# Four quarters of an MLP projection by seven products instead of eight, in a cross-attention kernel on one core

## The chip, the core and the metric

The kernel runs on one core of one Trainium2 chip. Such a core has TensorE (PE, the matmul array), VectorE (DVE), ScalarE (ACT), GpSimd (POOL) and SyncE (SP), which in this kernel only issues DMAs. Each engine runs its own instructions in the order in which the program gives them, and waits on semaphores for what others make. SBUF holds tiles of 128 partitions, PSUM the results of matmuls in eight banks of 128x512 fp32.

The metric is the device time of one execution in microseconds (us). A profile is one execution recorded by the hardware. Its span is the time between the first and the last recorded instruction, somewhat less than the time of the execution.

## The reference

One transformer block of cross-attention and MLP, in fp32, for 4 batches of 512 rows of 512 features, a context of the same shape, and 16 heads of 32 features:

```python
x = layer_norm(hidden_states, ln1_w, ln1_b)
q = x @ q_w + q_b ; k = ctx @ k_w + k_b ; v = ctx @ v_w + v_b      # 16 heads of 32
attn = softmax(where(mask, q @ k.T / sqrt(32), min))
hidden = (attn @ v) @ cproj_w + cproj_b + hidden_states
y = layer_norm(hidden, ln2_w, ln2_b)
return hidden + gelu(y @ fc_w + fc_b) @ proj_w + proj_b            # 512 -> 2048 -> 512
```

## The kernel before

**Units and blocks.** The attention is cut into 16 units w, each a batch (w // 4) and a group of four heads, and each unit into two halves of 256 query rows: 32 blocks p, and with each a pair (unit, half) of softmaxes. `block` runs eight score products (`scores`, line 317), then for each of them `soften`: VectorE reads the scores from PSUM and finds the extreme value (line 323), ScalarE takes exp (line 327). VectorE transposes the results (`turn`, line 335), takes reciprocals of the sums (line 354), ScalarE spreads them (`rr`, line 356) and VectorE transposes them too (line 360). `exchange` then moves the pair between partitions, by four GpSimd copies (line 393) and twelve DMAs on SP's queue (line 398), as soon as the buffer is free. `attend` of that pair (32 products of line 415) runs two blocks later, ahead of that block's scores.

**Fills.** VectorE and ScalarE need longer for a block's softmax than TensorE for its scores. So the list `put(p, ...)` gives each block other TensorE work, which `fill` issues at three points of the block: the first two take what fits in a budget of `CHAIN` = 3.4, the third takes all that is left. Such work is K, Q and V of later units (`prep_k`, line 255; `prep_q`, line 267; `prep_v_pair`, line 298), the output projection `cproj` (line 455), and the MLP of batches 0 and 1, taken in the order of the list `products` by `some(n)`. After the blocks come the last projection of the attention and what is left of the MLP.

**The MLP.** `fc` makes 2048 hidden features in pairs of 128, each pair by seven products over blocks of 128x256 (`fc_seven`, line 646; Strassen's scheme in Winograd's form, which saves one of eight products and adds sums of operands and results). Sums of fc's weights are made by GpSimd ahead of time (`fc_sums`, lines 597 and 600). The gelu of a pair (line 667) isn't issued with the pair but put into a list, `S["gelu"]`, that is emptied later: by the next pair's products, by a `proj` that needs it, or behind the `rr` copy of a block that has no pair in it. `proj` takes the hidden features in four quarters q of 512; each quarter has four row tiles t, of four matmuls 128x512 each, whose result VectorE adds to the row tile of the residual (line 709):

```python
for k in range(FQ):
    nc.tensor.matmul(acc, gT[q % 2][:, k, ts(t, P)], S["pw", b, q * FQ + k], ...)
h = S["hid", b, t]
nc.vector.tensor_tensor(h, acc, h, ALU.add)
```

Batch 1's first two quarters run by the same `proj`; the rest of the MLP runs behind the blocks.

**Weights.** `ptt` has twelve slots of 128x512: six for score tiles (`score_tile`), and six for the weights of K, Q and V, two slots for each (`kqv_w`); `load_w(w + 2)` follows a unit's last use of a slot. `pbt` holds eight weights of the MLP in turn, for which `load_mlp` (line 589) issues DMAs in the order of the list `weights`, as slots come free. All of these go through SP's queue, in the order of the program, like the DMAs of the exchange; a DMA that waits for its slot holds up those behind it. `store_rn` and `load_rn` (line 213) send the two rows of the layer norm's statistics through HBM and spread them over the partitions.

Of the kernel before, what the change touches and what calls it, by code (L numbers as in the profile page):

```python
# [20 lines left out]
P = 128  # L21
# [8 lines left out]
NQ = 4  # L30
# [4 lines left out]
FIRST = 2  # L35
IN_G = (1, 3, 5, 7)
IN_XE = (25, 27, 29, 31)

BY_ROW = ((1, 1), (1, 3))
BY_ACT = ((1, 2),)  # L40
# [11 lines left out]
def xattn_block(ctx: ExitStack, tc: tile.TileContext, x, rawT, encT, mask, q_w, k_w, v_w, c_w, fc_w, p_w, vecs, rows, out):  # L52
# [6 lines left out]
    const, keep, hids, tiles, small = pools(ctx, const=1, keep=1, hids=4, tiles=4, small=4)  # L59
# [28 lines left out]

    ys = const.tile([P, 3, 2, L // 2], F32, tag="ys", name="ys")
    wsum = const.tile([P, 2, 3, 2, P], F32, tag="wsum", name="wsum")  # L90

    def k_q(w, i):
        n = w % 4 * 2 + i
# [15 lines left out]
        return ptt[:, n * D : (n + 2) * D]  # L109

    def kqv_w(w, i):
        n = 4 * i + 2 + w % 2
        return ptt[:, n * D : (n + 1) * D].rearrange("p (d f) -> p d f", d=ND)

    S = {"gelu": []}
# [92 lines left out]
            )  # L208

    def load_rn(b):  # L210
        S["rows", b] = [hids.tile([P, L], F32, tag="hid2", bufs=2, name=f"rn_{b}_{i}") for i in range(2)]
        for i in range(2):
            nc.sync.dma_start(out=S["rows", b][i], in_=S["rn", b][i : i + 1, :].broadcast_to([P, L]))

# [25 lines left out]
    def load_w(w, queue=None, names=("wk", "wq", "wv")):  # L240
# [4 lines left out]
        for i, (n, src) in enumerate((("wk", k_w), ("wq", q_w), ("wv", v_w))):  # L245
            if n in names:
                S[n, w] = kqv_w(w, i)
                (queue or Q[0]).dma_start(out=S[n, w], in_=src[:, g, :, :])

    def prep_k(w):  # L250
        b, g = divmod(w, NG)
        kT = k_q(w, 0)
        acc = acc_tile(f"acck_{w}")
        for d in range(ND):
            nc.tensor.matmul(acc, S["wk", w][:, d, :], eT[:, d, :], start=(d == 0), stop=(d == ND - 1))  # L255
        load_w(w + 2, names=("wk",))
        nc.scalar.activation(kT, acc, AF.Identity, bias=vec[:, KB + g : KB + g + 1], scale=1.0)
        S["kT", w] = kT

    def prep_q(w):  # L260
        b, g = divmod(w, NG)
        qT = k_q(w, 1)
        parts = [slice(0, L)] if w else [slice(0, 2 * P), slice(2 * P, L)]
        for c in parts:
            acc = acc_tile(f"accq_{w}_{c.start}")[:, c]
            for d in range(ND):
                nc.tensor.matmul(acc, S["wq", w][:, d, :], xT[:, d, c], start=(d == 0), stop=(d == ND - 1))  # L267
            nc.scalar.activation(qT[:, c], acc, AF.Identity, bias=qb[:, g : g + 1], scale=-scale)
        load_w(w + 2, names=("wq",))
        S["qT", w] = qT  # L270

    def prep_v(w):
# [12 lines left out]
        if w:  # L285
            v_bias(w)

    def prep_v_pair(w):
        pair = range(w, w + 2)
        for u in pair:  # L290
            S["v", u] = five.tile([P, NT, P], F32, tag="v", name=f"v_{u}")
        n = 10
        wv = ptt[:, n * D : (n + 2) * D].rearrange("p (g d f) -> p d g f", g=2, d=ND)
        for i in range(2):
            acc = acc_tile(f"accv_{w}_{i}").rearrange("p (t g f) -> p t g f", t=2, g=2)
            for t in range(2):
                for d in range(ND):
                    nc.tensor.matmul(  # L298
                        acc[:, t], eT[:, d, ts(2 * i + t, P)], wv[:, d], start=(d == 0), stop=(d == ND - 1)
                    )  # L300
            for g, u in enumerate(pair):
                nc.scalar.copy(S["v", u][:, 2 * i : 2 * i + 2], acc[:, :, g])
        for u in pair:
            load_w(u + 2, names=("wv",))
            v_bias(u)

    def v_bias(w):
        v, bias = S["v", w], row[:, 2, ts(w % NG, P)]
# [123 lines left out]
    def load_h(b, *ts_):  # L432

        if ("xa", b) not in S:
            S["xa", b] = dram.tile([L, D], F32, tag=f"xa{b}", name=f"xa{b}")
        for t in ts_:
            if b == B - 1:

                S["h", b, t] = k_q(t // 2, t % 2)
            else:  # L440
                pool, tag, n = (tiles, "xn", 4) if not stays(b, t) else (hids, "hid2", 2) if b else (hids, "hid", 4)
                S["h", b, t] = pool.tile([P, D], F32, tag=tag, bufs=n, name=f"h_{b}_{t}")
# [93 lines left out]
    def load_hid(b, ts_):  # L536

        for t in ts_:
            if ("hid", b, t) not in S:
                S["hid", b, t] = hids.tile([P, D], F32, tag="hid", name=f"hid_{b}_{t}")  # L540
# [24 lines left out]
    def fcs(b, *cs):  # L565
        return [("fc", b, c) for c in cs]

    def pjs(b, q, *ts_):
        return [("p", b, q, t) for t in ts_ or range(NT)]
# [8 lines left out]
    weights = [(*k, n) for k, n in last_use.items()]  # L578

    weights += [("p", SPLIT, FIRST * FQ + k, None) for k in range(MW)]  # L580

    def load_mlp():

        while count[0] < len(weights) and (count[0] < MW or weights[count[0] - MW][3] < count[1]):
            name, b, f, _ = weights[count[0]]
            w = mlp_w(count[0])
            if name == "fc":
                w = w.rearrange("p (d f) -> p d f", d=ND)
            Q[0].dma_start(out=w, in_=fc_w[:, f, :, :] if name == "fc" else p_w[ts(f, P), :])
            S[name + "w", b, f] = w  # L590
            count[0] += 1

    NP = NF // 2
# [104 lines left out]
        count[4] += 1  # L698
        load_mlp()

    def proj(b, q, t):
        gelus(q % 2)
        acc = acc_tile(f"accp_{b}_{q}_{t}")
        for k in range(FQ):
            nc.tensor.matmul(  # L705
                acc, gT[q % 2][:, k, ts(t, P)], S["pw", b, q * FQ + k], start=(k == 0), stop=(k == FQ - 1)
            )
        h = S["hid", b, t]
        nc.vector.tensor_tensor(h, acc, h, ALU.add)
        if q == NQ - 1:  # L710
            (nc.gpsimd if b == 0 else nc.sync).dma_start(out=out[b, ts(t, P), :], in_=h)
# [25 lines left out]
    def last_mlps():  # L737
# [197 lines left out]
        for b, pairs, new in (  # L935
# [43 lines left out]

            project(b, pairs, sums, turns, middle)  # L980
            if b == SPLIT:
                S["more"] = [hids.tile([P, D], F32, tag="hid2", bufs=2, name=f"more_{n}") for n in range(2)]
                S["more"] = [m.rearrange("p (c n) -> p c n", c=NP // 2) for m in (*S["more"], row[:, 2, :])]
                to_split.extend(w_sums(5, pt[:, 2]))


# [3 lines left out]
    def do(fn):  # L990
        return [(0.0, fn)]
# [10 lines left out]
            (CHAIN, lambda: prep_v(w)),  # L1002
        ]

    def V(w):
        return [(CHAIN, lambda: prep_v_pair(w))]

    def C(b):
        return [(CHAIN, lambda t=t: cproj(b, t)) for t in range(NT)]
# [63 lines left out]
    def some(n):  # L1073
# [4 lines left out]
        assert n == 0  # L1078
        return taken

    def hid_(b, *ts_):
        return do(lambda: load_hid(b, ts_))

# [20 lines left out]
    def put(p, *work, before=(), mid=()):  # L1104
# [54 lines left out]
    put(26, c[3:], do(lambda: attend(12, 0)), some(2))  # L1159
    put(27, some(3))  # L1160
    put(28, some(3))
    put(29, some(4))
    put(30, some(3), hid_(1, 2, 3))
    put(31, some(3))

    due = {p: (p - 2,) for p in range(10, 2 * NW)}
    due |= {p: (p - 3,) for p in range(3, 9)} | {9: (6,), 26: ()}
    for p in range(2 * NW):
        w, half = divmod(p, 2)
        if half == 0 and w and w % NG == 0:  # L1170
            make_mb(w // NG)
        run(ahead[p])
        for pair in due.get(p, ()):
            attend(*divmod(pair, 2))
        if p > 10:
            fc_sums()

        def fill(n, work=fills[p]):
# [70 lines left out]
```

## Time and profile before

| | us |
|---|---|
| median of 3 runs | 762.17 (761.72 to 762.34) |
| the profiled execution, its own time | 760.67 |
| its span | 758.9 |
| TensorE busy | 753.9 |
| VectorE busy | 613.4 |
| GpSimd busy | 339.7 |
| ScalarE busy | 337.6 |

The page of the profile names instructions by line of the kernel (L705 is line 705), engine, operation and tile: `accp<-pbt,gt` is the product of `proj` from weights in `pbt` and hidden features in `gt`. In a timeline or in the chain of waits the first column is the start and the second the length in us; "x32" is the number of records; an fp32 matmul leaves two. A bracket at the end of a row holds the idle time of the engine ahead of the instruction, and what ended it. In the rows of the DMA queues "SPq" is the issue of a DMA by SP, not its transfer.

### The profile page before, as it was taken

To read this page: it belongs to the slowest core of one execution; us is meant where nothing else is said; L and a number is where in the kernel's file an instruction comes from. 1 tells how busy PE (TensorE), PEld (TensorE's weight loads), DVE (VectorE), ACT (ScalarE), POOL (GpSimd) and SP (SyncE) were. 2 spreads that over 40 slices of the span, in tenths; PEclk is the share of its full clock that TensorE was granted. 3 is DMA by queue.
4 is the path that set the end of the run, shared out by engine and by line. 5 is a ranking of instruction groups with operands and counts; after the bars stand their busy time and mean duration, and the time that the engine had idled before them with its cause. 6 is when DMAs were issued, how large, how long until landed. Compare 5 with 4: busy or idle time off the path is not lost.

```text
span 758.9 us, 13040 instructions
## 1 busy us (share of the span) xinstructions
PE 753.9 (99%) x4418; PEld 517.8 (68%) x4418; DVE 613.4 (81%) x1222; ACT 337.6 (44%) x768; POOL 339.7 (45%) x352
## 2 busy tenths in 40 slices
PE   9999999999999999999999999999999999999998
PEld 6655555567574545475454566468888899988997
DVE  3889999879995777887887989949877986956865
ACT  2566766565873574647753567501302221022200
POOL 1549447368664873244575444432050004403153
PEclk9999999999999999999999999999999999999999
DMA  9989889467897776665756867776724402046001
GB/s 329 341 255 247 207 207 257 104 199 200 220 243 229 223 231 177 184 175 129 177 133 186 214 194 193 172 227 215 260 98 135 167 26 91 30 146 214 1 15 43
DMA packets 60577, 134.59 MB, mean 177 GB/s; under 512 B 11312, under 2 KB 17072, under 8 KB 60384
## 3 DMA queue, kind: packets, MB, share of 16 engines
q1 hardware_dynamic: 58448, 126.73, 58.4%
q0 software_dynamic: 1920, 7.01, 2.7%
q8 instruction: 35, 0.57, 0.3%
q14 instruction: 30, 0.25, 0.1%
q10 hardware_dynamic: 144, 0.02, 0.0%
HBM read 69.23 MB, written 11.02 MB: 106 GB/s over the span
## 4 chain that ended last, share of the span: by engine, by line
PE 99%; POOL 0%; issue 0%; DVE 0%; DVEq 0%; POOLq 0%
PE q L646 26%; PE accp L705 11%; PE r L792 10%; PE sc L317 8%; PE av L415 8%; PE acck L255 8%; PE accq L267 8%; PE accc L455 6%; PE accv L278 5%; PE accv L298 3%; PE q1p L853 2%; PE tp L166 1%; PE warm L1044 1%; PE q3p L835 0%; PE q5p L835 0%; PE q4p L835 0%
## 5 line engine op out<-in xcount | busy, mean ns | idle before, releaser
L327 ACT ACTIVATE ptt<-ptt,mn 128x512 f32<-128x512 f32 x256 | 181.7, 711 | 142.8 <-DVE mn L323 142.8
L323 DVE CUSTOM_DVE_ANT_0 ptt<-sc,mb 128x512 f32<-128x512 f32 x256 | 160.6, 682 | 19.9 <-PE sc L317 19.8
L335 DVE STREAM_TRANSPOSE tb<-ptt 128x1024 f32<-128x1024 f32 x128 | 153.3, 1217 | 0.0
L393 POOL COPY pT<-tb 32x1088 f32<-32x1088 f32 x96 | 104.5, 1089 | 83.5 <-DVE oT L420 34.6
L705 PE MATMUL accp<-pbt,gt 128*128 128x512 f32 x192 | 85.3, 596 | 0.0
L646 PE MATMUL q<-yT,gt 128*128 128x256 f32 x320 | 78.9, 379 | 0.0
L667 ACT ACTIVATE ga<-ga,vec 128x512 f32<-128x512 f32 x40 | 26.7, 714 | 93.3 <-DVE ga L600 93.3
L646 PEld LDWEIGHTS q<-yT,gt 128*128 128x128 f32 x320 | 60.8, 190 | 8.1
L705 PEld LDWEIGHTS accp<-pbt,gt 128*128 128x128 f32 x192 | 35.9, 190 | 44.6 <-issue 39.1
L317 PE MATMUL sc<-pbt 32*128 32x512 f32 x512 | 64.7, 614 | 0.0
L646 PE MATMUL q<-ys,gt 128*128 128x256 f32 x240 | 61.6, 379 | 0.0
L255 PE MATMUL acck<-xe,ptt 128*128 128x512 f32 x128 | 59.0, 604 | 0.0
L267 PE MATMUL accq<-xe,ptt 128*128 128x512 f32 (+1 forms) x136 | 58.4, 575 | 0.0
L646 PEld LDWEIGHTS q<-ys,gt 128*128 128x128 f32 x240 | 45.7, 190 | 6.1
L600 DVE TENSOR_TENSOR ga<-q,ga 128x512 f32<-128x512 f32 (+1 forms) x60 | 36.2, 603 | 16.3 <-PE q L646 13.5
L327 ACT ACTIVATION_READ_ACCUMULATOR ptt<-ptt,mn 128x1 f32 x256 | 47.8, 187 | 0.0
L415 PE MATMUL av<-pT,v 128*32 128x256 f32 x768 | 46.4, 382 | 0.0
L267 PEld LDWEIGHTS accq<-xe,ptt 128*128 128x128 f32 x136 | 24.9, 190 | 31.4 <-issue 22.8
L255 PEld LDWEIGHTS acck<-xe,ptt 128*128 128x128 f32 x128 | 23.8, 193 | 30.8 <-issue 24.0
L317 PEld LDWEIGHTS sc<-pbt 32*128 32x128 f32 x512 | 26.9, 184 | 24.8 <-issue 16.9
L455 PE MATMUL accc<-wc,oT 128*128 128x512 f32 x96 | 42.5, 598 | 0.0
L278 PEld LDWEIGHTS accv<-ptt,xe 128*128 128x128 f32 x320 | 37.0, 192 | 4.9 <-DVE mn L323 2.7
(231 smaller groups left out, 1270.4 us busy)
## 6 DMA issues: line engine op xcount, KB each, us to landing
pT<-tb SPq DMA_DIRECT2D x288, 136.0 KB, 2.4
pbt<-p_w_dram SPq DMA_DIRECT2D x40, 256.0 KB, 3.3
gt<-ws SPq DMA_DIRECT2D x20, 512.0 KB, 3.3
gt<-tb SPq DMA_DIRECT2D x48, 136.0 KB, 3.8
xe<-tb SPq DMA_DIRECT2D x48, 136.0 KB, 2.5
pbt<-fc_w_dram SPq DMA_DIRECT2D x24, 256.0 KB, 4.7
gt<-fc_w_dram SPq DMA_DIRECT2D x20, 256.0 KB, 3.3
ptt<-k_w_dram SPq DMA_DIRECT2D x16, 256.0 KB, 4.2
```

The costliest lines, as they stand in the source:

```text
L255: nc.tensor.matmul(acc, S["wk", w][:, d, :], eT[:, d, :], start=(d == 0), stop=(d == ND - 1))
L267: nc.tensor.matmul(acc, S["wq", w][:, d, :], xT[:, d, c], start=(d == 0), stop=(d == ND - 1))
L317: nc.tensor.matmul(S["sc", w, qt][h], qT[r, ts(qt, P)], kT[r, :], start=True, stop=True)
L323: nc.vector.tensor_tensor_reduce(out=s, in0=S["sc", w, qt][h], in1=S["mb", w // NG], scale=1.0, scalar=FMAX, op0=ALU.add, op1=ALU.min, acc ...
L327: nc.scalar.activation(s, s, AF.Exp, bias=mn, scale=-1.0, accum_out=S["sums", w][:, qt, h : h + 1])
L335: nc.vector.transpose(tv[:, qt % 2, 2 * k : 2 * k + 2], S["ps", w, qt, k])
L393: nc.gpsimd.tensor_copy(pT[ts(i, HD), i], tb[ts(i, HD), i])
L415: nc.tensor.matmul(av[ts(h, HD), : 2 * P].rearrange(shape, **kw), v[:, t, ts(h, HD)], p[t][h], start=(t == 0), stop=(t == NT - 1),)
L455: nc.tensor.matmul(acc, S["oT", b][:, g, ts(t, P)], wc[:, g, :], start=(g == 0), stop=(g == NG - 1))
L646: nc.tensor.matmul(o, x[:, k], y[:, k], start=(k == 0), stop=(k == 1))
L705: nc.tensor.matmul(acc, gT[q % 2][:, k, ts(t, P)], S["pw", b, q * FQ + k], start=(k == 0), stop=(k == FQ - 1))
L792: nc.tensor.matmul(r, x[:, c], w[:, c], start=(c == 0), stop=(c == NP // 2 - 1))
```

## The change

Batch 0's `proj` is now computed by seven products over blocks too. With the hidden features of a quarter in blocks a11 to a22 (two steps of features by 256 rows) and the weights in blocks w11 to w22 (two steps by 256 columns), `proj_sums` makes four sums on GpSimd, and `proj` runs in three parts: products q1, q5, q2, then q7, q6, then q3, q4. Each product is four matmuls 128x256. Four more sums are made by GpSimd in part 0; two results go by ScalarE into blocks that are no longer needed; the products are joined to the residual by VectorE and GpSimd.

```diff
+    def proj_sums(b, q):
+        gelus(q % 2)
+        a11, a21, a12, a22, w11, w12, w21, w22, x, y = proj_blocks(b, q)
+        add(nc.gpsimd, x, a21, a22)
+        sub(y, w12, w11, nc.gpsimd)
+        sub(a21, a11, a21, nc.gpsimd)
+        sub(w12, w22, w12, nc.gpsimd)
...
+    def proj(b, q, part):
+        if b:
+            proj_whole(b, q, part)
+            return
+        a11, a21, a12, a22, w11, w12, w21, w22, x, y = proj_blocks(b, q)
+        def product(name, a, w):
+            o = acc_half(f"{name}_{b}_{q}")
+            for t in range(2):
+                for k in range(2):
+                    nc.tensor.matmul(o[:, t], a[:, k, ts(t, P)], w[:, k], start=(k == 0), stop=(k == 1))
+            return o
+        def join(engine, i, j, src):
+            h = hid4[:, 2 * i : 2 * i + 2, ts(j, HL)]
+            add(engine, h, src, h)
+        if part == 0:
+            q1 = product("q1j", a11, w11)
+            nc.scalar.copy(w11, q1)
+            if (b, q) in FOUND1:
+                join(nc.vector, 0, 0, q1)
+            q5 = product("q5j", x, y)
+            sub(x, x, a11, nc.gpsimd)
+            sub(y, w22, y, nc.gpsimd)
+            if (b, q) in FOUND5:
+                join(nc.vector, 0, 1, q5)
+                join(nc.vector, 1, 1, q5)
+            else:
+                nc.scalar.copy(a11, q5)
+            q2 = product("q2j", a12, w21)
+            join(nc.vector, 0, 0, q2)
+            sub(a12, a12, x, nc.gpsimd)
+            sub(w21, w21, y, nc.gpsimd)
+        elif part == 1:
+            q7 = product("q7j", a21, w12)
+            q6 = product("q6j", x, y)
+            add(nc.vector, y, q6, w11)
+            add(nc.vector, a21, q7, y)
+            late = () if (b, q) in FOUND1 else ((0, 0, w11),)
+            if (b, q) not in FOUND5:
+                late += (0, 1, a11), (1, 1, a11)
+            for i, j, src in late:
+                join(nc.gpsimd, i, j, src)
+        else:
+            q3 = product("q3j", a12, w22)
+            join(nc.vector, 0, 1, q3)
+            q4 = product("q4j", a22, w21)
+            join(nc.vector, 1, 0, q4)
+            for i, j, src in ((1, 1, a21), (0, 1, y), (1, 0, a21)):
+                join(nc.gpsimd, i, j, src)
+            if q == NQ - 1:
+                for t in range(NT):
+                    nc.gpsimd.dma_start(out=out[b, ts(t, P), :], in_=S["hid", b, t])
+        count[1] += 1
+        load_mlp()
```

`FOUND1 = ((0, 0),)` and `FOUND5 = ((0, 0), (0, 3))` name the quarters in which VectorE adds q1 or q5 out of PSUM straight to the residual. The sums x and y live in slots 3 and 7 of `ptt` (10 and 11 for quarter 3). For that, the weights of K and Q have one slot from unit 10 on, and the load of the next unit's weight follows the unit's own products:

```diff
+SINGLE = 10
-        n = 4 * i + 2 + w % 2
+        n = 4 * i + 2 + (w % 2 if i == 2 or w < SINGLE else 0)
...
+    def next_w(w, name):
+        if w != SINGLE - 1:
+            load_w(w + (2 if w < SINGLE else 1), names=(name,))
```

The residual's row tiles of batch 0 and two others come to lie in constant tiles `hid4` and `hid2` instead of a pool. The bias of V of unit 10 is held back until block 16's `attend` (`held_back`). The list `weights` has batch 1's proj weights at its end. The order of the products and the fills are laid anew:

```diff
-    products += fcs(SPLIT, 0) + pjs(0, 3) + fcs(SPLIT, 1, 2, 3) + pjs(SPLIT, 0) + pjs(SPLIT, 1)
+    products += fcs(SPLIT, 0) + pjs(0, 3, 0) + fcs(SPLIT, 1) + pjs(0, 3, 1, 2) + fcs(SPLIT, 2)
+    products += pjs(SPLIT, 0, 0) + fcs(SPLIT, 3) + pjs(SPLIT, 0, 1, 2, 3) + pjs(SPLIT, 1)
...
-    put(14, [q], some(2), x1)
-    put(15, x2[:1], V(10), x2[1:2], do(lambda: load_raw(3)), some(2), do(lambda: store_rn(3)), some(1),
-        do(lambda: load_rn(3)), some(1))
+    put(14, [q], some(2), x1, pre(0, 0))
+    put(15, some(1), x2[:1], V(10, True), x2[1:2], do(lambda: load_raw(3)), some(2), do(lambda: (store_rn(3), load_rn(3))))
...
-    put(18, [q], some(2), [k])
+    put(18, [q], some(2), pre(0, 1))
+    k12 = k
     k, q, v = A(13)
-    put(19, some(2), [k])
-    put(20, [q], stat(1, 0, 1), some(2))
+    put(19, [k12], some(1), [k], stat(1, 0, 1))
+    put(20, [q], some(2))
...
-    put(22, [k, q], norm(1, 0, 1), some(2), norm(1, 2, 3))
+    put(22, [k, q], norm(1, 0, 1), some(2), norm(1, 2, 3), pre(0, 2))
-    put(23, some(1), [k15], t2, pb_(1), some(1), h_(2, 2, 3, 0, 1))
+    put(23, some(1), [k15], t2, pb_(1), h_(2, 2, 3, 0, 1))
...
-    put(25, c[:3])
-    put(26, c[3:], do(lambda: attend(12, 0)), some(2))
-    put(27, some(3))
-    put(28, some(3))
-    put(29, some(4))
-    put(30, some(3), hid_(1, 2, 3))
+    put(25, c[:3], some(1))
+    put(26, c[3:], do(lambda: attend(12, 0)), some(1))
+    put(27, some(3), mid=pre(0, 3))
+    put(28, some(4))
+    put(29, some(3))
+    put(30, some(3), mid=hid_(1, 2, 3))
     put(31, some(3))
...
-    run(some(2) + do(c[1]) + stat(2, 2, 3) + rs(2) + cb(B - 1) + norm(2, 0, 1) + some(1) + do(c[2]))
+    run(some(1) + do(c[1]) + stat(2, 2, 3) + rs(2) + cb(B - 1) + norm(2, 0, 1) + some(1) + do(c[2]))
```

`some(n)` counts an fc pair as two and a part or tile of proj as one. So block 27 now holds fc pair (1,0) (batch 1, pair 0) and part 0 of quarter 3, block 28 pair (1,1) and parts 1 and 2, block 29 pair (1,2) and batch 1's first proj tile p10_0, block 30 pair (1,3) and p10_1, and block 31 p10_2, p10_3 and p11_0 (batch 1, quarter 1, tile 0). `pre(b, q)` runs `proj_sums`; with `mid=` it stands in the middle of the block's softmax instead of at a fill.

More of the change, by code (lines that the diff above doesn't have):

```diff
@@ L37 @@
 IN_XE = (25, 27, 29, 31)
+SINGLE = 10
+FOUND1, FOUND5 = ((0, 0),), ((0, 0), (0, 3))
 BY_ROW = ((1, 1), (1, 3))
@@ L210, in load_rn @@
     def load_rn(b):
-        S["rows", b] = [hids.tile([P, L], F32, tag="hid2", bufs=2, name=f"rn_{b}_{i}") for i in range(2)]
+        S["rows", b] = [hid2[:, i] for i in range(2)]
         for i in range(2):
@@ L440, in load_h @@
             else:
-                pool, tag, n = (tiles, "xn", 4) if not stays(b, t) else (hids, "hid2", 2) if b else (hids, "hid", 4)
-                S["h", b, t] = pool.tile([P, D], F32, tag=tag, bufs=n, name=f"h_{b}_{t}")
+                S["h", b, t] = (
+                    (hid2 if b else hid4)[:, t] if stays(b, t)
+                    else tiles.tile([P, D], F32, tag="xn", name=f"h_{b}_{t}")
+                )
             Q[0].dma_start(out=S["h", b, t], in_=x[b, ts(t, P), :])
@@ L577, in xattn_block @@
         last_use |= {(name, b, f): done - 1 for f in range(i * n, (i + 1) * n)}
-    weights = [(*k, n) for k, n in last_use.items()]
+    weights = [(*k, n) for k, n in last_use.items() if k[:2] != ("p", SPLIT)]
+    weights += [(*k, n) for k, n in last_use.items() if k[:2] == ("p", SPLIT)]
     weights += [("p", SPLIT, FIRST * FQ + k, None) for k in range(MW)]
@@ L699, in fc_by_pair, with proj_blocks, proj_whole @@
         load_mlp()
-    def proj(b, q, t):
+    def proj_blocks(b, q):
+        g = gT[q % 2]
+        w = [pbt[:, n * D : (n + 2) * D].rearrange("p (k f) -> p k f", k=2) for n in
+             (S["pw", b, q * FQ + k] for k in (0, 2))]
+        a11, a21, a12, a22 = (g[:, 2 * k : 2 * k + 2, ts(i, HL)] for k in range(2) for i in range(2))
+        w11, w12, w21, w22 = (w[k][:, :, ts(j, HL)] for k in range(2) for j in range(2))
+        x, y = (
+            ptt[:, n * D : (n + 1) * D].rearrange("p (k l) -> p k l", k=2)
+            for n in ((10, 11) if (b, q) == (0, NQ - 1) else (3, 7))
+        )
+        return a11, a21, a12, a22, w11, w12, w21, w22, x, y
+    def proj_sums(b, q):
[5 more added lines that the diff above has]
+        sub(w12, w22, w12, nc.gpsimd)
+    def proj_whole(b, q, t):
         gelus(q % 2)
@@ L981, in last_mlps @@
             if b == SPLIT:
-                S["more"] = [hids.tile([P, D], F32, tag="hid2", bufs=2, name=f"more_{n}") for n in range(2)]
-                S["more"] = [m.rearrange("p (c n) -> p c n", c=NP // 2) for m in (*S["more"], row[:, 2, :])]
+                S["more"] = [
+                    m.rearrange("p (c n) -> p c n", c=NP // 2) for m in (hid2[:, 0], hid2[:, 1], row[:, 2, :])
+                ]
                 to_split.extend(w_sums(5, pt[:, 2]))
```

36 lines of the change are left out of this document (22 added, 14 removed).

## The prediction

> **What bounds the kernel now.** I read the page's busy shares and clock line first, then the chain of waits, then TensorE's own waits.
>
> ```profile
> span 758.9 us, 13040 instructions
> ...
> PE 753.9 (99%) x4418; PEld 517.8 (68%) x4418; DVE 613.4 (81%) x1222; ACT 337.6 (44%) x768; POOL 339.7 (45%) x352
> ...
> PEclk9999999999999999999999999999999999999999
> ...
> PE 99%; POOL 0%; issue 0%; DVE 0%; DVEq 0%; POOLq 0%
> ```
>
> TensorE is busy for 753.9 of 758.9 us at full clock, and the chain that ends last is TensorE alone. So a microsecond of products taken away is a microsecond of time, and so is each microsecond in which TensorE waits for an operand; the other engines' work costs nothing until it is late. The stage table shows it in the blocks too (columns: stretch, length, then busy us with instruction counts of PE, PEld, DVE, ACT and POOL, then clock and DMA share): PE fills both stretches, while POOL has 87 us free in the first and 39 in the second.
>
> ```profile
> 218.90:416.70 197.80, 197.79 (x1048) 107.00 (x1040) 156.33 (x336) 112.69 (x261) 110.44 (x115) 1.00 0.69 187
> 416.70:489.30 72.60, 72.60 (x425) 42.66 (x417) 66.95 (x142) 46.84 (x104) 33.71 (x38) 1.00 0.72 192
> ```
>
> **What the change takes from TensorE.** The chain shows one quarter of proj as a single stretch, and, from the end of the kernel, products of the 128x256 shape that the seven products use. An fp32 matmul is two records.
>
> ```profile
> 228.24 13.73 PE accp L705 x32
> ...
> 545.31 3.45 PE q2p L835 x16
> ```
>
> A quarter today is 4 tiles x 4 steps = 16 matmuls 128x512, 32 records, 13.73 us (0.429 each). After it is 7 products x 2 row halves x 2 steps = 28 matmuls 128x256, 56 records at 3.45/16 = 0.2157: 12.08 us. Saved: 1.65 a quarter, **6.6 us** for batch 0's four. This is the only gain; nothing in TensorE's products is taken away elsewhere.
>
> **What it adds off TensorE.** GpSimd: 32 sums of operands and 3, 6, 6 and 4 joins in the four quarters, 51 of 128x512. VectorE: 25 joins in place of 16. ScalarE: 6 copies out of PSUM.
>
> ```profile
> 379.04 4.97 POOL L426 TENSOR_TENSOR h<-h,row 128x512 f32<-128x512 f32 x4
> ...
> L709 DVE TENSOR_TENSOR h<-accp,h 128x512 f32<-128x512 f32 x20 | 13.5, 679 | 12.1 <-PE accp L705 12.1
> ...
> L857 ACT COPY p1p<-q1p 128x512 f32<-128x512 f32 x3 | 1.8, 585 | 10.4 <-PE q1p L853 10.4
> ```
>
> That is 51 x 1.24 = 63 us of GpSimd, 9 x 0.68 = 6 of VectorE, 6 x 0.59 = 3.5 of ScalarE. Over quarters 0 to 2, whose parts lie in blocks 15, in 19 and 20, and in 23, 25 and 26, the free time above covers it, and I cost it at nothing: the four sums ahead of a quarter (5.0 us) stand at the end of blocks 14, 18 and 22, behind GpSimd's softmax copies, and are wanted in the next block. Were the copies of a pair's softmax pushed back by all four, the av products that read them would be up to 5 us late; GpSimd's order puts the sums behind that block's copies. The moved statistics, the held-back bias of V(10) (two GpSimd additions behind the attend of block 16), the moved row tiles and the constant tiles in place of a pool are hidden in the same way. What is left are five places where something wanted by TensorE has no slack.
>
> **Wait A: quarter 3, block 27.** Its five GpSimd sums and joins come in one block with fc pair (1,0) ahead of them. Rows of blocks 26 to 28 of the chain, of VectorE and of GpSimd:
>
> ```profile
> 408.10 7.06 PE accp L705 x16
> 415.17 1.86 PE av L415 x32
> 417.03 1.93 PE sc L317 x16
> 418.96 6.24 PE q L646 x28
> 425.20 3.43 PE accp L705 x8
> ...
> 412.17 0.40 DVE L360 STREAM_TRANSPOSE tb<-rr 128x256 f32<-128x256 f32 x1
> ...
> 412.77 4.47 POOL L393 COPY pT<-tb 32x1088 f32<-32x1088 f32 x4 [2.37 <-PE accp L705]
> ...
> 428.19 0.72 POOL L600 TENSOR_TENSOR wsum<-pbt 128x256 f32<-128x256 f32 x1 [10.95 <-DMA pbt<-fc_w_dram]
> 430.50 0.72 POOL L597 TENSOR_TENSOR wsum<-pbt,wsum 128x256 f32<-128x256 f32 x1
> ```
>
> Keep block 26's clock. In place of the 7.06 us at 408.10 stand q3 and q4 of quarter 2 (16 records, 3.45): to 411.55. av and sc take 3.80 (415.17 to 418.96), fc pair (1,0) 6.24: to 421.6; q1 (8 records, 1.73): to 423.3, where q5 wants x and y. GpSimd: the last transpose of block 26 ends at 412.57, and VectorE's part-1 joins before it put that 0.6 later, 413.2; q3's and q4's joins (0.65 each) end at 414.5. GpSimd's last joins follow, to 416.3 (1.24 for the two that must wait for them, partly ahead), then the four copies of the pair, 4.47, to 420.8, the sums of fc pair (1,1), 3.03 (428.19 to 431.22), to 423.8, and x and y, 2.48, to 426.3. The wait is 426.3 - 423.3 = **3.0**. Between: 2.4 if VectorE is not late, 4.0 if the joins follow one after the other. Behind it TensorE's whole queue waits, and no DMA.
>
> **Wait G1: block 29.** p10_0's third step needs the gelu of fc pair (1,1), which ScalarE runs behind the row-sum copy of the block that follows. Block 30 of today has the same layout, sc, seven products, one proj tile:
>
> ```profile
> 461.20 2.06 PE sc L317 x16
> 463.27 6.24 PE q L646 x28
> 469.51 3.43 PE accp L705 x8
> ...
> 470.81 0.40 ACT L356 COPY rr<-rsum 128x256 f32<-128x256 f32 x1 [0.33 <-DVE rsum L354]
> 471.50 1.28 ACT L667 ACT_TABLE_LOAD   x1
> 472.80 1.34 ACT L667 ACTIVATE gt<-gt,vec 128x512 f32<-128x512 f32 x2
> ```
>
> Today the tile at 469.51 needs a gelu of a block earlier. After, the third step is due two steps in, at 469.51 + 1.72 = 471.22, and the first gelu ends at 472.80 + 0.67 = 473.47: **2.25** (to 2.6 if the pattern runs a little late, 2.0 if it runs early; the softmax before it is paced from sc, so it does not go away).
>
> **Wait G2: block 31.** p11_0, third tile of the block, needs the gelu of fc pair (1,3):
>
> ```profile
> 474.81 2.13 PE sc L317 x16
> 476.94 10.50 PE accp L705 x24
> ...
> 486.72 1.33 ACT L667 ACTIVATE gt<-gt,vec 128x512 f32<-128x512 f32 x2
> ```
>
> Two tiles end at 476.94 + 7.0 = 483.94, the third step is due at 485.65, the gelu ends at 486.72 + 0.67 = 487.39: **1.7** (1.5 to 2.0).
>
> **K of unit 13, block 19.** From unit 10 a weight has one slot, so k_w(13) is issued once K of unit 12 has run, behind the block's twelve exchange DMAs. Block 16 has that pattern:
>
> ```profile
> 244.41 7.91 SPq L398 DMA_DIRECT2D pT<-tb  x12
> ...
> 252.41 0.53 SPq L248 DMA_DIRECT2D ptt<-k_w_dram  x1
> ...
> 245.77 3.63 PE acck L255 x8
> ...
> DMA to landing us min/median/max: 2.5/5.1/5.8
> ...
> ptt<-k_w_dram SPq DMA_DIRECT2D x16, 256.0 KB, 4.2
> ...
> DMA  8967993899997295686200000000000595789999
> ```
>
> The fourth row is of line 248's loads of all weights, the fifth of k_w's alone (its median), the last the DMA engines' busy tenths in 40 slices from 252 to 262. K begins at 245.77, k_w goes out 6.64 later and lands 9.1 later at the shortest landing, 2.5. It is wanted after K (3.63) and a part 0 (24 records, 5.18): 8.8. I take 0.3, by the shortest landing, because the wire falls silent by 257.25: k_w and the q_w behind it are both in within 4.8 us, so the first of them in about half of that. The bounds are 0 and 3.6 (landing 5.8).
>
> **Small waits.** In block 15 the store and load of the layer-norm rows, and pair 15's exchange, move on SP's queue behind four p_w loads of 0.4 us of issue each; the av of block 17 stands behind them. I take 0.3, with bounds 0 and 1.8 (`L589`, four issues):
>
> ```profile
> 240.42 0.82 SPq L213 DMA_DIRECT2D rn<-rn  x2
> 241.34 1.79 SPq L589 DMA_DIRECT2D pbt<-p_w_dram  x4
> ```
>
> For banks that wait on joins in blocks 26 and 27 I take 0.2 (bounds 0 and 0.65, one join).
>
> **The sum.** -6.6 + 3.0 + 2.25 + 1.7 + 0.3 + 0.5 = **+1.15**. The profiled execution took 760.67 (its span is 758.9, the rest lies around it), so 761.8; the median of the runs, 762.17, is 1.50 above it, so 762.17 + 1.15 = **763.3**; I say 763.4, +0.16%. With the bounds of the three larger waits alone (2.4 + 2.0 + 1.5 to 4.0 + 2.6 + 2.0) the sum runs from +0.1 to +2.8, so 762.3 to 765.0.
>
> **The clock after a wait.** The longest wait of TensorE today is one of 1.4 us at the start, and the clock line above never drops after it. What a slow clock costs is seen in the warm-up: 18 records of 128x128 in 4.21 us, 0.234 each, where 336 of that shape in r take 0.112 each.
>
> ```profile
> PE warm L1044 <- POOL ident masks.py:199: 1.4, 1, 1.4
> ...
> 1.35 4.21 PE warm L1044 x18
> ...
> 717.77 37.53 PE r L792 x336
> ```
>
> The sum above has nothing for it, since A is taken at 3.0; were the warm-up's slowness to come back once, 18 x (0.234 - 0.112) = 2.2 us would be lost. [...]
>
> **Rivals.** *The gain stays, A is gone.* GpSimd may clear in time: if the joins and fc sums of (1,1) are done before the copies (they need a free GpSimd while pair 26's softmax is still open; POOL is free there for 2.37 us today) then x and y end by 423.3. Then -6.6 + 2.25 + 1.7 = -2.65 and 759.5. For it: the 39 us free in that stretch. Against: five items of GpSimd in series, each bound to VectorE's end. *K of unit 13 late.* If k_w lands at its group's median, 5.1 instead of 2.5, in block 19, the wait is 2.9 instead of 0.3; at 4.2, the median of k_w alone, 2.0. So +1.7 to +2.6 on the forecast: 765.5. It decides once the landing passes 2.2 us. For it: the median. Against: the loads of that group issued early in the kernel are on a busier wire. *Slow clock.* If A comes out at its upper bound, 4.0, as long as the warm-up's whole stretch, and the slow clock with it, A costs 1.0 more and the clock 2.2: 766.6. For it: every step of A's series on GpSimd waits for the one before. Against: the value taken is 3.0, and 1.4 us left the clock alone. *The change doesn't do what it says*, that is, TensorE runs more than the 56 records a quarter: the order of the changed kernel's products has 28 matmuls a quarter, so 6.6 us stand.
>
> **How the numbers follow.** What a measurement of this kernel can tell from no change is about 0.2%, 1.5 us: below 760.65 is faster, above 763.7 slower. The forecast gets 0.45 (0.26 of it inside, 0.19 above 763.7), A gone 0.18, K late 0.17, slow clock 0.08, and the rest 0.12 (0.02 faster, 0.06 the same, 0.04 slower): faster 0.20, same 0.32, slower 0.48. The range 759.0 to 767.0 takes in all the cases with half a microsecond beside the outer ones, and leaves out A and G1 gone together below, and K at its longest landing with the slow clock above; the forecast's own range is 762.3 to 765.0.
>
> **What would show it.** In the profile after: quarters of 12.1 us in 56 records on the chain; a wait of TensorE ahead of q5 in block 27 released by GpSimd's y, of 2.4 to 4.0; one of 2.0 to 2.6 and one of 1.5 to 2.0 ahead of proj tiles, released by ScalarE's gelu; at K of unit 13 one below 0.5 released by a DMA; the clock line unbroken at 9. Wrong, if TensorE waits for GpSimd in blocks 15 to 23 too (then the cover counted as free is not), or if A is absent.

## The result: slower by 0.8%

| | before | after |
|---|---|---|
| median us (lowest to highest, 6 runs each) | 761.87 (760.99 to 762.34) | 768.12 (765.42 to 770.42) |
| the profiled execution: time, span | 760.67, 758.9 | 768.06, 766.3 |
| ratio of the times | | 1.0082 (95%: 1.0062 to 1.0102) |

The time lies above the forecast of 763.4 and above the range of 759.0 to 767.0. The page of the changed kernel, the lines that answer to those of before, and TensorE's waits (engine and line, released by whom: total us, times, longest us):

```profile
span 766.3 us, 13324 instructions
...
PE 751.8 (98%) x4514; PEld 535.9 (70%) x4514; DVE 620.7 (81%) x1231; ACT 340.4 (44%) x774; POOL 403.3 (53%) x403
...
PE 35%; ACT 0%; DVE 0%; DVEq 0%; issue 0%
```

```profile
PE acck L263 <- DMA ptt<-k_w_dram: 3.6, 1, 3.6
PE accp L744 <- DMA pbt<-p_w_dram: 2.4, 3, 1.3
PE q5j L763 <- POOL ptt L614: 1.9, 1, 1.9
PE accp L744 <- ACT gt L684: 1.6, 1, 1.6
PE warm L1132 <- POOL ident masks.py:199: 1.4, 1, 1.4
```

TensorE is busy 2.1 us less and the span is 7.4 longer. The chain of waits covers only 35% of the span: followed back from the end, it stops at a gelu for which TensorE waited in block 31. Four waits are new, 9.5 us together: K of unit 13 in block 19, q5 of quarter 3 in block 27, p10_0 in block 29 and p11_0 in block 31. All four places are in the prediction. The two proj tiles waited as long as it says; K's wait came out at its upper bound, and q5's below its lower one. The saving is there: in this stretch of TensorE's timeline (start, length, operation) each product begins 1.73 us behind the last, so a quarter of seven takes 12.1.

```profile
444.62 1.89 PE L763 MATMUL q7j<-pbt,gt 128*128 128x256 f32 x8
446.34 1.89 PE L763 MATMUL q6j<-ptt 128*128 128x256 f32 x8
448.07 1.89 PE L763 MATMUL q3j<-pbt,gt 128*128 128x256 f32 x8
```

**Block 19.** TensorE's, SP's and GpSimd's timelines:

```profile
293.09 3.70 PE L263 MATMUL acck<-xe,ptt 128*128 128x512 f32 x8
...
300.08 1.89 PE L763 MATMUL q2j<-pbt,gt 128*128 128x256 f32 x8
305.58 5.37 PE L263 MATMUL acck<-xe,ptt 128*128 128x512 f32 x8 [3.61 <-DMA ptt<-k_w_dram]
```

```profile
291.81 8.71 SPq L411 DMA_DIRECT2D pT<-tb  x12
300.94 10.37 SPq L252 DMA_DIRECT2D ptt<-k_w_dram  x2
```

```profile
299.74 0.56 POOL L706 DMA_DIRECT2D ws<-wsum  x1 [0.30 <-POOL wsum L614]
300.30 0.54 POOL L707 DMA_DIRECT2D ws<-pbt  x1
```

K of unit 12 begins at 293.09, k_w(13) goes out 7.85 later (6.64 was taken from block 16 of before) and TensorE gets it 4.6 after that (2.5 was taken). Just ahead of it GpSimd sends 512 KB of fc sums to HBM. And K of unit 13 then takes 5.37 us where K of unit 12 took 3.70. The table of stretches shows why (TensorE's busy time stands after the length; third from the end is the granted clock, the share of full speed at which TensorE was let run):

```profile
303.19:306.61 3.42, 1.03 (x3) 0.58 (x4) 1.16 (x4) 1.79 (x4) 2.61 (x3) 1.00 0.37 133
306.61:310.02 3.41, 3.41 (x6) 1.35 (x5) 0.00 (x0) 0.00 (x0) 0.00 (x0) 0.50 0.00 0
310.02:313.43 3.41, 3.41 (x43) 1.50 (x45) 0.42 (x1) 1.97 (x2) 0.01 (x1) 1.00 0.22 77
```

For 3.41 us the clock is halved, right behind a stretch of the same length in which TensorE was busy for 1.03. That costs 1.7. Two groups of score products, those of blocks 4 and 26, take longer too:

```profile
68.81 2.81 PE L330 MATMUL sc<-pbt 32*128 32x512 f32 x16
405.54 2.70 PE L330 MATMUL sc<-pbt 32*128 32x512 f32 x16
```

Before they took 2.00 and 2.04. The first varies from one execution to the next: in the profiles of the experiments, whose block 4 is the same, it takes 2.00 to 3.44. The second is 2.70 in all of them. The sum for the 7.4 by which the span grew: -6.6 saved; waits 3.6, 1.9, 2.4 and 1.6; the halved clock 1.7; the score products 1.5: together 6.1. The other 1.3 isn't traced to single places.

### The profile page after: what moved, and what is told of

It is laid out like the page before. It is cut to its first block, busy times and chain, and to the rows that moved or that the text cites. A ratio compares the mean times of both kernels' runs of the same rounds, so it can differ in the third digit from the quotient of the medians.

```text
span 766.3 us, 13324 instructions
## 1 busy us (share of the span) xinstructions
PE 751.8 (98%) x4514; PEld 535.9 (70%) x4514; DVE 620.7 (81%) x1231; ACT 340.4 (44%) x774; POOL 403.3 (53%) x403
## 5 line engine op out<-in xcount | busy, mean ns | idle before, releaser
L263 PE MATMUL acck<-xe,ptt 128*128 128x512 f32 x128 | 60.7, 618 | 3.6 <-DMA ptt<-k_w_dram 3.6
L439 POOL TENSOR_TENSOR hid<-hid,row 128x512 f32<-128x512 f32 x18 | 23.5, 1332 | 39.9 <-DMA hid<-xa 39.8
L322 POOL TENSOR_TENSOR v<-v,row 128x512 f32<-128x512 f32 x16 | 20.3, 1280 | 40.6 <-ACT v L291 33.3
```

## The experiments

Each starts from the changed kernel ("as changed" below), and ratios are to the kernel before, run on the same chip. As changed, the ratio is 1.0062 to 1.0102. The intervals of e1, e2, e3, e5 and e8 overlap that one, so what each of them gained alone rests on the waits in its profile, which is one execution, and not on its time.

**e1: another queue for k_w(13).**

```diff
-            load_w(w + (2 if w < SINGLE else 1), names=(name,))
+            queue = nc.scalar if (w, name) == (12, "wk") else None
+            load_w(w + (2 if w < SINGLE else 1), queue, names=(name,))
```

> The weight of K of unit 13 is issued by ScalarE's queue right behind K of unit 12, not by SP's behind the twelve exchange DMAs of the block. In the changed kernel it went out 7.85 us after K began and TensorE waited 3.61 us for it; then the clock was granted at 0.5 for 3.41 us. Theory (place in the queue): it goes out about 3.7 us after K begins, lands before the 8.8 us at which it is wanted, the wait is 0, the clock stays at 1.00, and the time falls by 3.6 + 1.75 = 5.4, to about 762.7. Rival (the wire, which GpSimd's store of the fc sums and the exchange share): the landing takes over 5 us and a wait of 1 us or more stays; time about 765. Second rival (the slow clock has nothing to do with the wait): the wait goes, a window of 0.5 stays somewhere, time about 764.5.

Measured: 767.99 (8 runs), ratio 1.0078 (1.0048 to 1.0109). ScalarE's timeline, then TensorE's:

```profile
300.70 0.71 ACT L341 ACTIVATE ptt<-ptt,mn 128x512 f32<-128x512 f32 x1
300.96 0.33 ACTq L252 DMA_DIRECT2D ptt<-k_w_dram  x1
```

```profile
294.09 3.70 PE L264 MATMUL acck<-xe,ptt 128*128 128x512 f32 x8
305.70 3.67 PE L264 MATMUL acck<-xe,ptt 128*128 128x512 f32 x8 [2.73 <-DMA ptt<-k_w_dram]
```

The issue stands behind ScalarE's exps of the block, so k_w goes out 6.9 after K of unit 12 began: 1.0 earlier than as changed, where 4.2 earlier was expected. The wait is 2.7 instead of 3.6, less by about as much. From its issue to its use k_w still takes 4.7, on a queue that it doesn't share with the exchange. So the place on SP's queue isn't what makes the landing late.

**e8: the stores out of the way.** GpSimd's sums of an fc pair and their stores at the end of block 19.

```diff
-        if p > 10:
+        if p > 10 and p != 19:
             fc_sums()
...
-    put(19, [k12], some(1), [k], stat(1, 0, 1))
+    put(19, [k12], some(1), [k], stat(1, 0, 1), do(fc_sums))
```

> As changed, but in block 19 GpSimd's sums of an fc pair, and the two stores of them to HBM (512 KB), come at the end of the block instead of ahead of K of unit 13. Theory (the late landing has two halves, the place on SP's queue and the shared wire): k_w goes out at the same place but lands in some 2.5 us instead of 4.6, and the wait falls from 3.6 to about 1.5; no window of slow clock follows it; time about 764.5. Rival (the queue alone): the wait stays between 3 and 4 and the time at 768.

Measured: 765.29 (9 runs), ratio 1.0052 (1.0028 to 1.0076). TensorE's and SP's timelines:

```profile
301.62 1.89 PE L763 MATMUL q2j<-pbt,gt 128*128 128x256 f32 x8
304.37 3.67 PE L263 MATMUL acck<-xe,ptt 128*128 128x512 f32 x8 [0.87 <-DVE hid L617]
```

```profile
293.34 7.88 SPq L411 DMA_DIRECT2D pT<-tb  x12
301.65 0.34 SPq L252 DMA_DIRECT2D ptt<-k_w_dram  x1
```

k_w goes out 7.0 after K of unit 12 began (294.63) and is in within 2.7. The wait is 0.9 instead of 3.6 (the row puts its end down to a sum of VectorE, so k_w may have come earlier still), K of unit 13 takes 3.67, and the mean granted clock of this execution is 1.000. The stores, with the sums that move with them, are what makes the landing late: from the issue of k_w to K of unit 13 it takes 4.6 to 5.2 in all six profiles with K of unit 12 in block 19 and the stores ahead (as changed, e1, e2, e3, e4, e6), and 2.7 and 2.8 in the two with the stores moved (this one and e11, below). The late issue isn't explained by them: the twelve DMAs of the exchange take 8.4 to 8.9 on SP's queue in those six, 7.9 here, but 8.6 in e11.

**e5: K of unit 12 back in block 18.**

```diff
-    put(18, [q], some(2), pre(0, 1))
-    k12 = k
+    put(18, [q], some(2), [k], pre(0, 1))
...
-    put(19, [k12], some(1), [k], stat(1, 0, 1))
+    put(19, some(1), [k], stat(1, 0, 1))
```

> One part of the change undone: K of unit 12 back in block 18, all else as changed. The weight of K of unit 13 can then be loaded a block ahead. Theory: the wait in block 19 (2.7 to 4.2 us in five profiles) goes and with it the window of slow clock that follows it in most of them: time 768.1 - 3.6 - 1.7 x 0.6 = about 763.5. Rival (the wait only moves, to the weight of Q of unit 13 or to block 18, whose products now stand 3.6 us longer ahead of the exchange): time above 766.

Measured: 765.64 (12 runs), ratio 1.0051 (1.0028 to 1.0073): half the expected gain. The wait of K is gone and another stands in its place:

```profile
302.10 3.60 PE L263 MATMUL acck<-xe,ptt 128*128 128x512 f32 x8
308.80 2.58 PE L428 MATMUL av<-pT,v 128*32 128x256 f32 x32 [3.10 <-DMA ptt<-k_w_dram]
```

```profile
295.53 9.23 SPq L411 DMA_DIRECT2D pT<-tb  x12
```

Block 19 is now K of one unit and a part 0, and over early: the last DMA of pair 18's exchange goes out at 304.8, and av is wanted at 305.7. The row names k_w's load as what ended the wait, but av doesn't read that weight; it reads `pT`, which the exchange writes. That it waits for the exchange is argued from this and from the times, not shown. The rival was right that the wait moves, but not to Q's weight. As changed, the second K fills this time.

**e2: quarter 3's sums first in block 27.**

```diff
-        if p > 10:
+        if p > 10 and p != 27:
             fc_sums()
...
-    put(27, some(3), mid=pre(0, 3))
+    put(27, some(3), mid=pre(0, 3) + do(fc_sums))
```

> In block 27 GpSimd makes the four sums of quarter 3 ahead of the sums of fc pair (1,1). Theory (the series on GpSimd is what q5 waits for): x and y end 2.9 us earlier, the wait of 1.88 goes, and the time falls by 1.9, to about 766.2. Rival (the gain is lost at the next pair, whose sums now end 5 us later): a wait of TensorE before the products of pair (1,1) in block 28, and a time of about 768.

Measured: 766.08 (9 runs), ratio 1.0053 (1.0033 to 1.0074). The wait of q5 is not among TensorE's waits any more, and none came in block 28; the time fell by 2.0, as expected.

**e3, e4, e6: the two waits of p10_0.** e3 issues the gelus earlier, e4 puts back the old order of the weights' loads, e6 has e3's gelus, p10's weights on ScalarE's queue, and a gelu of one column that loads its table in time.

```diff
-    put(28, some(4))
+    put(28, some(4), do(gelus))
...
-    put(30, some(3), mid=hid_(1, 2, 3))
+    put(30, some(3), do(gelus), mid=hid_(1, 2, 3))
```

> The gelu of fc pairs (1,1) and (1,3) is issued at the end of blocks 28 and 30 instead of in the next block behind the softmax. Theory: the wait of 1.64 in block 31 goes; the 2.42 in block 29 stay, since the weights of p10 land later than the gelu is needed: time 768.1 - 1.6 = 766.5. Rival (the wait in block 29 was the gelu's, whatever the releaser's name): that one goes too, time about 764.1.

```diff
-    weights = [(*k, n) for k, n in last_use.items() if k[:2] != ("p", SPLIT)]
-    weights += [(*k, n) for k, n in last_use.items() if k[:2] == ("p", SPLIT)]
+    weights = [(*k, n) for k, n in last_use.items()]
```

> Only the order of the loads of MLP weights is put back to that of the kernel before, so that the weights of p10 go out ahead of those of fc pair (1,3), about 1.1 us earlier. Theory (two waits lie over each other in block 29): the wait at the first step of p10_0 shrinks from 1.30 to about 0.2, and the one at its third step, for the gelu, grows from 0.73 to about 2: together 2.2 to 2.4 as before, time unchanged at about 768. Rival (the loads alone): the wait falls to below 0.5, time about 766.

```diff
+            queue = nc.scalar if (name, b) == ("p", SPLIT) and f < FQ else Q[0]
-            Q[0].dma_start(out=w, in_=...)
+            queue.dma_start(out=w, in_=...)
...
     gelus()
+    nc.scalar.activation(warm_g, nhalf[:, :1], AF.Gelu_apprx_tanh)
```

> The early gelus of e3_gelu, with a gelu of one column behind block 31 that loads its table in good time, and the four loads of p10's weights on ScalarE's queue, idle there, instead of behind the twelve exchange DMAs on SP's. Theory (block 29 has two waits that lie over each other, and only both removed gain): both waits of TensorE for p10 go, and so do the 1.64 of block 31 and the 1.31 before q1p of e3_gelu: 768.1 - 2.4 - 1.6 = 764.1. Rival (the wire, with GpSimd's four stores of the output on it): the wait at p10 stays at 1 us or more, time 765.5.

Measured: e3 767.89 (5 runs), ratio 1.0078 (1.0066 to 1.0090); e4 781.78 (4 runs), 1.0268 (1.0248 to 1.0287); e6 764.09 (12 runs), 1.0023 (1.0004 to 1.0041). The waits of p10_0 as changed, in TensorE's timeline; ScalarE's gelu that it needs, two halves of 0.67; then e3's waits; then e4's timeline and waits; last the same tile in e6, with no wait ahead of it:

```profile
463.02 1.10 PE L744 MATMUL accp<-pbt,gt 128*128 128x512 f32 x2 [1.30 <-DMA pbt<-p_w_dram]
464.51 1.10 PE L744 MATMUL accp<-pbt,gt 128*128 128x512 f32 x2 [0.39 <-DMA pbt<-p_w_dram]
466.33 1.96 PE L744 MATMUL accp<-pbt,gt 128*128 128x512 f32 x4 [0.73 <-DMA pbt<-p_w_dram]
```

```profile
465.14 1.33 ACT L684 ACTIVATE gt<-gt,vec 128x512 f32<-128x512 f32 x2
```

```profile
PE accp L744 <- DMA pbt<-p_w_dram: 2.2, 4, 1.3
...
PE q1p L940 <- ACT ga L684: 1.3, 1, 1.3
```

```profile
467.61 1.98 PE L743 MATMUL accp<-pbt,gt 128*128 128x512 f32 x4 [2.48 <-ACT gt L683]
```

```profile
PE accp L743 <- DMA pbt<-p_w_dram: 11.4, 1, 11.4
```

```profile
460.66 3.60 PE L745 MATMUL accp<-pbt,gt 128*128 128x512 f32 x8
```

| waits at p10_0, us | weights | gelu | together |
|---|---|---|---|
| as changed | 2.4 | behind the weights | 2.4 |
| e3, gelu early | 2.2 | 0 | 2.2 |
| e4, weights early | 0 | 2.5 | 2.5 |
| e6, both early | 0 | 0 | 0 |

Either cause alone makes the whole wait; only both removed gain. e6 fell by 4.0 as expected, 764.1. It has a price: with p10's weights on ScalarE's queue, the twelve exchange DMAs of block 29 take 14.3 us on SP's queue (8.9 as changed, 8.2 in e3). e3's gain at p11_0 (its 1.6 is gone) was lost for the most part to the 1.3 before q1p, where a gelu table is now loaded late (1.28 at 533.92; as changed there is no load between 500 and 560); e6, which loads it early, has no such wait. e3's time didn't fall, where 766.5 was expected. e4's time was expected at 768; it has a wait of 11.4 that was not foreseen, for weights of a later tile of proj, and a lower mean clock (0.984 to 0.989 in its runs, 0.993 to 1.000 as changed): this part of the change is needed where the tiles now stand. Why the old order makes those weights so late wasn't followed up.

**e7 and e11: all together.** e7 is e2 + e5 + e6. e11 is e2 + e6 with K of unit 12 in block 19 as changed, and GpSimd's sums and stores at the end of blocks 14 and 19.

> All four together: K of unit 12 in block 18, quarter 3's sums ahead of those of fc pair (1,1), and the two edits of e6_gelu_pw. Theory (the saving of 6.6 is whole and the waits are all that stood against it): no wait of TensorE over 1 us but the one at the start, clock 1.00, time 761.9 - 6.6 + 1.5 for banks and switches = 756.8, faster than the kernel before by 0.6%. Rival (part of the saving was never there, since short products cost more between them): no waits and still above 758.5.

> The kernel of e7_all once more, as the base of the next two on the same chip: about 759, clock 0.999 to 1.000, no window of slow clock in block 27.

```diff
-        if p > 10:
+        if p > 10 and p not in (14, 19, 27):
             fc_sums()
...
-    put(14, [q], some(2), x1, pre(0, 0))
+    put(14, [q], some(2), x1, pre(0, 0), do(fc_sums))
...
-    put(19, [k12], some(1), [k], stat(1, 0, 1))
+    put(19, [k12], some(1), [k], stat(1, 0, 1), do(fc_sums))
```

> K of unit 12 as in the change, in block 19, but the sums of fc weights and their stores at the end of blocks 14 and 19, and the edits to blocks 27 to 31 of e7_all. Theory (late landings come from the stores on the shared wire): the waits of 1.9 ahead of block 15's av and of 0.5 and 1.1 in block 20 seen in e7_all's profile go, a wait of about 1 us at K of unit 13 stays: time about 757.5, 1.5 below e7_all. Rival (other transfers make them late): 759 or more.

Measured: e7 759.17 (12 runs), ratio 0.9965 (0.9947 to 0.9983), and once more 757.41 (6 runs), 0.9934 (0.9909 to 0.9960); e11 757.52 (7 runs), 0.9937 (0.9914 to 0.9959). Both beat the kernel before. Of e7's two expectations neither holds: its profiles still have waits of about 2 us, and its two medians lie on both sides of 758.5. Rows of TensorE's timeline (e7's first profile, then e11's):

```profile
219.91 1.93 PE L428 MATMUL av<-pT,v 128*32 128x256 f32 x32 [1.91 <-POOL gt L615]
```

```profile
304.45 3.67 PE L263 MATMUL acck<-xe,ptt 128*128 128x512 f32 x8 [1.63 <-DMA ptt<-k_w_dram]
461.85 1.93 PE L428 MATMUL av<-pT,v 128*32 128x256 f32 x32 [1.68 <-DVE gt L618]
```

In e7 the av products of block 15 wait 1.9, and 2.1 in its second profile; in e11 that wait is gone, as its theory says. So are the 0.5 ahead of block 20's av and the late scores behind it, but there K of unit 12 has changed its place too. K's wait of 1.6 is there instead, and the av of block 30, which waited 0.7 in e7's first profile and not at all in the second, waits 1.7. These rows name work on `gt` as what ended the av's waits, but av doesn't read `gt` there; that it waits for the exchange that writes `pT` is argued, not shown. Whether e11 is better than e7 can't be told: 757.5 as expected, but e7 on the same chip took 757.4 (759.2 on the other).

**e9 and e10: longer waits, and the clock behind them.** e7, with the first of quarter 3's sums made more often than once.

```diff
-        add(nc.gpsimd, x, a21, a22)
+        for _ in range(3 if (b, q) == (0, 3) else 1):
+            add(nc.gpsimd, x, a21, a22)
```

That is e9; e10 has 4 for 3.

> e7_all, where GpSimd makes the first of quarter 3's sums three times instead of once, so that x and y come 2.5 us later; TensorE had 1.0 us to spare there and now waits 1.5. That is at most 0.44 of a window of 3.41 us. Theory (the clock is halved for a window of 3.41 us where TensorE stood idle for about half of the window before; shares of 0.49 to 0.57 have been seen on both sides): no slow window in block 27, time e7_all + 1.5. Rival (an idle stretch of a whole window is needed): the same.

> The same with four times instead of once: x and y 3.7 us later, a wait of 2.7. That is 0.40 to 0.79 of the fuller one of the windows that it falls into, over a half in about 8 of 10 runs, and never a whole window. Theory (about half a window idle): in most runs a window at 0.5 follows it, 1.7 us lost beside the wait; time e7_all + 2.7 + 0.8 x 1.7 = e7_all + 4.1, mean clock about 0.002 lower. Rival (a whole window): no slow window, e7_all + 2.7, clock as in e7_all.

Measured: e9 760.33, ratio 0.9993 (0.9965 to 1.0021), and e10 763.56, ratio 1.0023 (1.0005 to 1.0042), 12 runs each. That is 1.5 and 4.7 above the median of all 18 runs of e7 (758.85), but 2.9 and 6.2 above e7 on the same chip, so the times bear out the expected 1.5 and 4.1 only roughly. Between the two, on one chip, lie 3.2: 1.3 of longer wait, and 1.9 for which the clock is the likely cause. The stretches of block 27 in both, at the wait and behind it:

```profile
424.11:427.52 3.41, 2.12 (x10) 1.89 (x11) 3.17 (x7) 0.68 (x2) 3.41 (x4) 1.00 0.44 104
427.52:430.94 3.42, 3.42 (x44) 2.03 (x42) 1.92 (x4) 0.00 (x0) 3.26 (x6) 1.00 0.65 147
```

```profile
430.16:433.57 3.41, 1.11 (x5) 1.01 (x6) 2.87 (x6) 0.59 (x1) 3.41 (x3) 1.00 0.53 119
433.57:436.98 3.41, 3.41 (x10) 2.70 (x9) 1.29 (x2) 0.00 (x0) 3.33 (x5) 0.50 0.63 144
```

Behind e9's wait of 1.6 the clock was 1.00. Behind e10's of 2.9, with TensorE busy for 1.11 of the 3.41 us ahead, it was 0.50 for 3.41. e10's profile also has a wait of 3.4 ahead of block 20's av, of which the edit touches nothing; its execution was the slowest of the twelve, at a mean clock of 0.996. One stretch of 3.41 at 0.50 takes 0.002 off the mean of a span of 764.4 (an estimate from these numbers), so a second one is likely, not shown. The mean clock was 0.998 or lower in 9 of e10's 12 runs, in 3 of e9's and in 1 of e7's 18. The rival, a whole idle window, falls: e10's wait of 2.9 was enough.

## Why the prediction failed, step by step

- **What the change takes from TensorE**, 6.6 us: right. With most of the waits taken out, in e7, the kernel is faster than before by 0.35 and 0.66%, 2.7 and 5.0 us. In e7's first profile, -6.6 with the waits of 1.9, 0.7 and 0.5 and the score products of blocks 4, 20 and 26, which take 2.7 more than before, makes -0.8; its span is 758.1 beside 758.9. So the saving is whole there.
- **The covers costed at nothing** in blocks 15 to 23 held as far as GpSimd's sums go: as changed, no wait there but that of K. e7's waits of 1.9 and 2.1 in block 15 are gone in e11, where the fc sums and their stores come behind quarter 0's sums; whether GpSimd's sums have a part in them isn't shown. The small wait of 0.3 taken for block 17's av didn't come as changed, and was 0.2 to 0.6 in e3, e6 and e11. The score products of block 26 were 0.7 late, where up to 0.65 was allowed for the banks; those of block 4 (0.8) were not foreseen, and what makes either late wasn't tried.
- **Wait A**, 3.0: the mechanism is right (e2), the size was 1.9. The term that failed is VectorE's lateness. TensorE's and VectorE's timelines in block 26:

```profile
415.50 1.89 PE L763 MATMUL q4j<-pbt,gt 128*128 128x256 f32 x8
```

```profile
417.42 0.40 DVE L373 STREAM_TRANSPOSE tb<-rr 128x256 f32<-128x256 f32 x1
```

q4 ends at 417.2 (1.73 behind its start) and the last transpose at 417.8, 0.6 later; the sum had 411.55 and 413.2, 1.65 later. GpSimd's series begins that much earlier against TensorE. Block 26's late scores hold TensorE up by 0.7 just ahead; that they are the reason is likely, not shown. The rival with A gone was priced at 759.5 without the 0.8 that the forecast has for K and the small waits; with them it is 760.3.
- **G1**, 2.25: the gelu is as late as worked out (2.5 where it stands alone, in e4), but the weights of p10, which the prediction didn't list as a term, are late by as much. The two lie over each other, so the sum came out right, 2.4, and half of the reason was missing.
- **G2**, 1.7: right, 1.6, and gone in e3.
- **K of unit 13**, 0.3: this step failed, and it measured 3.6. The issue came 1.2 later than taken (7.85 after K began, not 6.64), and the landing took 4.6 instead of 2.5. Both were read from block 16, "because the wire falls silent by 257.25". In block 16 GpSimd works on the layer norm's rows behind its copies and has no such store; in block 19 it stores 512 KB just then, and with these stores out of the way the landing took 2.7 and 2.8 (e8, e11). What makes the issue late stays open. GpSimd's timeline of before:

```profile
244.40 4.47 POOL L393 COPY pT<-tb 32x1088 f32<-32x1088 f32 x4 [0.43 <-DVE oT L420]
248.96 10.38 POOL L218 TENSOR_TENSOR raw<-raw,rn 128x512 f32<-128x512 f32 x8
```

The wait came out at its upper bound, 3.6. The rival of a late k_w had the mechanism, but its price, 2.9, was below that bound.
- **The clock after a wait.** The prediction looked for the slow clock only behind wait A at its upper bound of 4.0, and made it a case of its own. It put the clock at nothing in its sum, with A at 3.0, and this failed too. No run of before shows behind which wait the clock falls, nor that the warm-up's slowness, from which 2.2 was worked out, is that of a slow clock: the profile of before has a granted clock of 1.00 there as well (1.35 to 5.56). What the runs showed in its place is 0.50 for 3.41 us: behind K's wait of 3.6 as changed, at a cost of 1.7, behind q5's of 2.9 in e10 and of 1.9 in e3. The two rivals, late K and halved clock, were counted as cases that exclude each other, 765.5 or 766.6; the two can come together (as changed they did; in e1, behind a wait of 2.7, K of unit 13 took 3.67, and in e3, behind one of 3.4, the clock was 1.00), and with both the sum is 763.4 + 3.3 + 1.7 - 1.1 (A) = 767.3, and 768.1 with the late scores of block 4. The prediction left K at its longest landing together with the slow clock out of its range. That is why the range ended too low.

## What to carry to other kernels

When a wait is sized by the same pattern in another block, compare what else is on the wire in both: here stores from another queue made the landing 4.6 us or more instead of 2.7 to 2.8. Waits on one instruction can lie over each other, and the releaser that the profile names is only the last; undo each alone and both together before one is called free. And a wait of TensorE can have a second price, the halved clock behind it (here 0.50 for 3.41 us behind waits of 1.9, 2.9 and 3.6, at a cost of 1.7 behind the last), so a change that trades products for waits can pay more than the sum of its waits.

## What the runs showed of the hardware

The granted clock fell to 0.50 behind some of TensorE's waits and stayed at 1.00 behind others. Two waits of e3's profile, the stretch that the wait ends in and the one behind it: first at K of unit 13, which waited 3.4, then at q5 of quarter 3, which waited 1.9.

```profile
303.57:306.99 3.42, 1.49 (x4) 0.81 (x5) 0.94 (x3) 1.55 (x3) 2.36 (x2) 1.00 0.29 110
306.99:310.40 3.41, 3.41 (x30) 1.44 (x32) 0.00 (x0) 1.18 (x2) 0.00 (x0) 1.00 0.05 11
426.45:429.86 3.41, 1.55 (x8) 1.04 (x7) 3.30 (x6) 1.56 (x5) 3.41 (x4) 1.00 0.36 96
429.86:433.27 3.41, 3.41 (x10) 2.70 (x9) 1.91 (x4) 0.00 (x0) 3.37 (x4) 0.50 0.79 181
```

| run | what waited | wait, us | clock behind it |
|---|---|---|---|
| as changed | K of unit 13 | 3.6 | 0.50 for 3.41 us |
| as changed | q5 of quarter 3 | 1.9 | 1.00 |
| as changed | p11_0 | 1.6 | 1.00 |
| e3 | K of unit 13 | 3.4 | 1.00 |
| e3 | q5 of quarter 3 | 1.9 | 0.50 for 3.41 us |
| e9 | q5 of quarter 3 | 1.6 | 1.00 |
| e10 | q5 of quarter 3 | 2.9 | 0.50 for 3.41 us |

So the length of the wait doesn't decide it alone: 1.9 stands on both sides, and 3.4 was followed by 1.00 where 2.9 was followed by 0.50. What else does isn't shown. Executions of one kernel differ in the clock too: as changed, 765.42 at a mean of 1.000 and 770.42 at 0.993.
